# x1 and x2 turned by block loads and VectorE transposes instead of TensorE transposes, with two buffers of turned probability blocks and rounds that begin with the output projection

## The chip, the core and the metric

The kernel runs on one core of one Trainium2 chip, written in Bass with Tile. The core has five engines with an instruction stream each: TensorE (PE in the profile; PEld is its loading of weights), VectorE (DVE), ScalarE (ACT), GpSimd (POOL) and SyncE (SP). DMAs are issued from the streams of SP and ACT. The metric is device microseconds of one execution, as the median of a few executions.

## The reference

One decoder layer in float32, for 8 x 512 positions of width 512. `x` is (8, 512, 512); below, index t = 0..7 of the first axis is called a tile. Three blocks follow each other, each with a residual and a layer norm behind it:

```python
x = layernorm(x + self_attention(x))      # relative positions, 16 heads of 32, over the axis of 8
x = layernorm(x + cross_attention(ctx, x, mask))
x = layernorm(x + ffn(x))

# cross_attention, for each t: 8 heads of 64
k, v   = split((ctx[t] @ W_src.T + b_src) * mask[t])      # ctx[t]: 512 x 1024
q      = (x1[t] @ W_tgt.T + b_tgt) * mask[t]
p      = softmax(q k.T / 8, masked keys at -inf)          # 8 x 512 x 512
update = p v
return concat([x1[t], update]) @ W_out.T + b_out

# ffn: 512 -> 2048 -> 512
h   = relu(x2 @ w1.T + b1)
out = fp16(fp8(h) @ fp8(w2).T + fp16(b2))
```

Here `x1` is the output of the first layer norm and `x2` that of the second.

## The kernel before

**First stage, 0 to 928 us of the span.** Self attention over the axis of 8 for all positions, and beside it the projections of the contexts. It leaves the rows of x1 in DRAM (`x1d`, one array per tile, position by feature) and the keys and values of the tiles in DRAM (`kd`, `vd`). The context of the last tile is projected later, in the pieces `psk`/`psv` of `project_context`. The diff does not touch this stage.

**Second stage, 928 us to the end: rounds 0 to 7.** Each round works on a tile t and on the tiles behind it. In round t TensorE's stream holds, in this order of meaning:

- cross attention of tile t, in eight units u = (t, c, jj): c is one of four pairs of heads, jj one of two pairs of 128-row groups;
- output projection `project_out(t-1, j)`, j = 0..3, into the bank `pox`: four products of the turned x1 (`x1Ts`, two halves used in turn) and four of the turned attention output (`uT`), lines 890 and 894, then on VectorE the addition of the residual (the natural rows `x1`) and the statistics of the layer norm;
- `finish(t-2, j)`: the second product of the feed forward net (line 1045, bank `o`), additions, statistics, and in the side work the last normalization and the store of the result;
- the queries of tile t+1: `turn` transposes x1 on TensorE through PSUM (`xtr`, line 741) and ScalarE copies it into `x1Ts` (line 742); `queries(t+1, o)` multiplies it with `w_tgt` (line 747, bank `psq`), and VectorE writes `qTx` (line 754);
- the hidden layer of tile t-1, `hidden_steps`: x2 is transposed in the same way into `x2T` (`x2tr`), `sums_of_b` adds and subtracts its quarters on VectorE into `tx` (four additions), and then for n = 0..7 seven half-size products replace eight (groups `hx`, `hy`, `hz`, line 967, each of two weights and one 256-wide operand a piece). Results are added on VectorE (line 1002 after step `p13`, line 1012 after `p6`, line 1021 after `p7`) and copied or put through relu on ScalarE (lines 982, 988, 1008, 1015). The weights of the step n, with their sums, come from DRAM (`w1d`) into a ring of three: `load_w1`, issued on ACT's queue. For the first tile they come from `w1T` in parts on SP's queue, are summed on GpSimd and stored.

**A unit of cross attention.** `scores` (line 767) multiplies queries and keys for two j and two heads. Four `exponentials` follow: VectorE adds the mask and takes the minimum (line 786), ScalarE exponentiates and sums (line 796). Two `divide` (lines 808 and 811) scale on VectorE. Two `turn_blocks` (line 823) transpose on VectorE: each 32 x 32 block of `pe` is turned and put in its place in `pb`, a buffer of 128 x 4096 floats that the two units of one c share. That turns blocks in themselves; the blocks must still change partition. `move_blocks` (line 836) does this with sixteen DMAs on SP's queue, 128 KB each, from `pb` to `pT`. Then `attend` multiplies `pT` with the values (line 870, bank `av`), and ScalarE copies to `uT`. pb_c, av_c and vx_c below are the buffer, the attention and the values of the pair c. Both pools have one buffer:

```python
        pbp = pool("pb", 1)
        ptp = pool("ptp", 1)
```

**What sets the order.** PE, VectorE, ScalarE and SP run in the order in which the Python code issues instructions (`manual_schedule`). `weave` mixes two lists: `dense` (projections, queries, hidden layer; each item with a cost in us) and the attention of the round (`attention_of`: each item with a weight and with the number of dense items that must have gone before, `begun`, `projected`, `queried`). Side work, which is nearly all of VectorE's and ScalarE's part of the attention, stands in two lists, `side` and `urgent`. `run(cost, step)` is called for every item: it first issues the moves that are due, then takes side work as far as a credit of 0.7 of the costs allows, then issues the step. `settle(tag)` issues side work up to a tag at once. `later` holds loads that wait for some more items (keys `load_k`, values `load_v`). `attend` may be issued when its blocks are turned. `run` holds back the `turn_blocks` of the next pb while a move is due or was issued less than 15 modelled us ago:

```python
                held = moves or clock < moved + MOVE
                if held and any(item[0][0] == "t" for item in free):
                    free = [item for item in free if item[0][0] not in "tT"]
```

In `attention_of` the attention of the pair c stands behind the scores of unit 2c+3 of the same tile; that of the last pair stands in the next round, behind three of the `finish` steps:

```python
                    dense += first
                    begun = len(dense)
                    dense += values_of(t - 1) + second + out4[0]
```

So a round t from 2 to 6 begins with o_0 to o_2 of tile t-2, then the last attention of tile t-1, o_3, the four pox, the first attention of tile t, psq_0 to psq_2, the transposes of x2, psq_3, and the hidden layer, with scores in between and the other two attentions in the hidden layer. Natural x1 rows (`load_x1`, four buffers) are loaded a round ahead, at the beginning of the round. Round 0 has the context pieces, the turn of tile 1 and the queries of tile 1; round 1 begins with the last two pieces, psv_2 and psv_3, and `take_ring`, which reuses the memory of `w_src` for the weights of the hidden layer.

## Time and profile before

| | us |
|---|---|
| median of 3 executions (2267.41 to 2281.33) | 2270.61 |
| the profiled execution | 2276.34 |
| its span, first to last instruction | 2274.5 |
| first stage, to 928.0 | 928.0, PE busy 878.8 |
| round 0, 928.0 to 1080.6 | 152.6, PE busy 132.5 |
| round 1, to 1258.5 | 177.9, PE busy 147.3 |
| rounds 2 to 6, to 1414.5, 1565.7, 1718.7, 1871.9 and 2016.3 | 156.0, 151.2, 153.0, 153.2 and 144.4 |
| round 7, to 2158.8 | 142.5, PE busy 123.6 |
| the end, to 2274.5 | 115.7, PE busy 104.7 |

Each border from 1080.6 on is the start of the first pox of a tile in TensorE's stream (round 0 is what lies before the first of them, the end what follows the last tile's first pox; what a round has ahead of its first pox counts to the window before); a window's row of the trace gives each engine's busy time in it. Of the span of 2274.5 us PE is busy 2099.1, VectorE 1515.0, ScalarE 583.6, GpSimd 166.5. The mean granted clock of TensorE is 0.965 of full speed. DMA moved 293.31 MB in 141,247 packets.

How to read the profile: a group of instructions is given by line, engine, operation and its tiles, output before input (`pb<-pe` writes a tile of the name pb from one named pe), with its partitions and elements, its count, busy us and mean ns of one. Behind the bar stands the idle time of the engine just before those instructions and what ended most of it. A timeline's row is start, length, engine, line and operation, with the wait ahead of it and its releaser in brackets; SPq is the issuing of DMAs on SP. In the chain of waits each row is start, length, and the engine or DMA that the end was waiting for at that time. A row of the DMA view gives packets, MB and the share of 16 engines' time in the window asked for.

### The profile page before, as it was taken

The numbers are of one execution on the slowest core, as the hardware profiler recorded it, in microseconds if no ns is written. First come the engines' busy times: TensorE is split into PE (matmuls) and PEld (weight loads), VectorE is DVE, ScalarE is ACT, GpSimd is POOL, SyncE is SP. The second block draws the span as 40 slices with busy tenths as digits, with TensorE's granted clock in tenths as the row PEclk, the third lists the DMA queues.
The fourth block names the chain that finished last, engine by engine and source line by source line (L and its number), as shares of the span: only waits on it lengthen the run. The fifth ranks groups of instructions, "written<-read, shape, count | busy, mean of one in ns | idle before, by whom it ended". The sixth has DMA issues, their size and how long they took to land.

```text
span 2274.5 us, 21753 instructions
## 1 busy us (share of the span) xinstructions
PE 2099.1 (92%) x7552; PEld 1224.5 (54%) x7552; DVE 1515.0 (67%) x2542; ACT 583.6 (26%) x1327; POOL 166.5 (7%) x156
## 2 busy tenths in 40 slices
PE   7999999999989999888986999999989999998798
PEld 5654674465457667433354455464554654645455
DVE  4799999989999993356453654656646557456324
ACT  2011102111111111222242343342433433424312
POOL 1000110110001010102111000000000000000000
PEclk9999999999999999998998999999999999999899
DMA  8130452163035237554555444464453544634512
GB/s 297 48 126 13 153 178 77 37 220 102 7 121 176 83 125 261 191 165 116 136 140 169 107 136 119 116 187 117 121 168 87 140 134 111 177 92 130 138 49 86
DMA packets 141247, 293.31 MB, mean 129 GB/s; under 512 B 18640, under 2 KB 47312, under 8 KB 141136
## 3 DMA queue, kind: packets, MB, share of 16 engines
q1 hardware_dynamic: 116848, 211.91, 32.3%
q10 hardware_dynamic: 24288, 80.00, 10.7%
q8 instruction: 60, 0.98, 0.2%
q14 instruction: 51, 0.42, 0.1%
HBM read 165.49 MB, written 59.24 MB: 99 GB/s over the span
## 4 chain that ended last, share of the span: by engine, by line
PE 63%; DVE 19%; DMA 12%; ACT 2%; SPq 2%; issue 1%; POOL 0%; DVEq 0%; ACTq 0%; POOLq 0%
PE px L539 7%; PE hx L967 7%; PE av L870 5%; PE pox L890 5%; PE pox L894 5%; PE o L1045 4%; PE s L767 4%; PE pz L539 4%; DVE pv L428 3%; DMA ffn<-w1d 3%; PE psq L747 3%; PE hz L967 3%; PE ps_q L338 3%; DMA pT<-pb 2%; PE po L454 2%; DVE pv L438 2%
## 5 line engine op out<-in xcount | busy, mean ns | idle before, releaser
L796 ACT ACTIVATE pe<-pe,nmax 128x512 f32<-128x512 f32 x256 | 182.7, 715 | 350.9 <-DVE nmax L786 349.6
L823 DVE STREAM_TRANSPOSE pb<-pe 128x512 f32<-128x512 f32 x256 | 162.3, 681 | 86.7 <-DMA pT<-pb 64.2
L786 DVE CUSTOM_DVE_ANT_0 pe<-s,mb 128x512 f32<-128x512 f32 x256 | 163.5, 681 | 42.7 <-PE s L767 41.0
L967 PE MATMUL hx<-ffn 128*128 128x256 f32 x512 | 144.1, 406 | 49.9 <-DVE tm L1021 49.7
L428 DVE TENSOR_TENSOR pv<-v,sc 128x2048 f32<-128x2048 f32 x64 | 148.5, 2321 | 2.0
L967 PE MATMUL hx<-x2T,ffn 128*128 128x256 f32 x512 | 140.4, 398 | 8.4 <-ACT ffn L1008 8.4
L379 DVE TENSOR_TENSOR pq<-qw,k 128x2048 f32<-128x2048 f32 x64 | 146.3, 2286 | 1.1
L388 DVE TENSOR_REDUCE sc<-pq 128x64 f32<-128x2048 f32 x64 | 146.0, 2282 | 1.4
L870 PE MATMUL av<-pT,vx 128*64 128x512 f32 x512 | 127.1, 642 | 20.8 <-DMA pT<-pb 18.4
L967 PEld LDWEIGHTS hx<-ffn 128*128 128x128 f32 x512 | 94.9, 199 | 88.9 <-DVE tm L1021 59.0
L767 PE MATMUL s<-kT,qTx 64*128 64x512 f32 x512 | 128.7, 621 | 0.0
L811 DVE TENSOR_SCALAR pe<-pe,rden 128x512 f32<-128x512 f32 x256 | 119.5, 509 | 4.5
L967 PEld LDWEIGHTS hx<-x2T,ffn 128*128 128x128 f32 x512 | 98.6, 198 | 40.9 <-ACT ffn L1008 16.3
L454 PE MATMUL po<-w_o,aoT 128*128 128x512 f32 x256 | 118.6, 606 | 0.7 <-ACT aoT L451 0.7
L338 PE MATMUL ps_q<-w_in,xt 128*128 128x512 f32 x256 | 116.7, 593 | 0.0
L890 PE MATMUL pox<-w_xo,x1Ts 128*128 128x512 f32 x256 | 116.0, 596 | 0.0
L747 PE MATMUL psq<-x1Ts,w_tgt 128*128 128x512 f32 x256 | 113.5, 596 | 2.0 <-ACT x1Ts L742 2.0
L894 PE MATMUL pox<-w_xo,uT 128*128 128x512 f32 x256 | 115.1, 592 | 0.0
L338 PE MATMUL ps_k<-w_in,xt 128*128 128x512 f32 x256 | 114.0, 593 | 0.0
L1045 PE MATMUL o<-w2q,hq 128*128 128x512 fp8e4 x480 | 113.6, 397 | 0.0
L338 PE MATMUL ps_v<-w_in,xt 128*128 128x512 f32 x256 | 111.6, 594 | 0.0
L1002 DVE TENSOR_TENSOR ffn<-hx,ffn 128x256 f32<-128x256 f32 x64 | 27.2, 424 | 95.5 <-ACT hq L1015 66.6
(180 smaller groups left out, 3160.9 us busy)
## 6 DMA issues: line engine op xcount, KB each, us to landing
pT<-pb SPq DMA_DIRECT2D x512, 128.0 KB, 2.5
ffn<-w1d ACTq DMA_DIRECT2D x56, 896.0 KB, 5.7
ch<-in_ctxT_dram SPq DMA_DIRECT2D x56, 256.0 KB, 3.3
td<-tx SPq DMA_DIRECT2D x28, 384.0 KB, 3.3
tx<-td SPq DMA_DIRECT2D x28, 384.0 KB, 5.6
r<-in_x_dram SPq DMA_DIRECT2D x32, 256.0 KB, 3.8
xt<-in_xT_dram SPq DMA_DIRECT2D x32, 256.0 KB, 2.7
x1d<-r ACTq DMA_DIRECT2D x32, 256.0 KB, 3.9
```

The costliest lines, as they stand in the source:

```text
L338: nc.tensor.matmul(ps, lhsT=xt[:, e, :], rhs=w_in[:, e, part * E : (part + 1) * E], start=(e == 0), stop=(e == EC - 1),)
L428: nc.vector.tensor_tensor(pr, v_all[:, :, fs].rearrange("p s (h d) -> p s h d", d=D1), sc[:, t, g * HH * T : (g + 1) * HH * T] .rearrange( ...
L454: nc.tensor.matmul(po, lhsT=aoT[:, c * P : (c + 1) * P], rhs=w_o[:, c, :], start=(c == 0), stop=(c == EC - 1),)
L539: nc.tensor.matmul(bank[:, first], lhsT=w7[:, a, f, ps] if part == 0 else b[f][:, ps], rhs=b[f] if part == 0 else w7[:, a, f, :], start=st ...
L747: nc.tensor.matmul(ps, lhsT=w_tgt[:, e, o * P : (o + 1) * P], rhs=x1T[t][:, e, :], start=(e == 0), stop=(e == EC - 1),)
L767: nc.tensor.matmul(ps[:, h, :], lhsT=qT[t][half[h], c, j * P : (j + 1) * P], rhs=kT[t, c][half[h], :], start=True, stop=True,)
L796: nc.scalar.activation(pe, pe, AF.Exp, bias=nmax[:, h : h + 1], scale=-1.0, accum_out=den[:, h : h + 1],)
L870: nc.tensor.matmul(av[half[h], :], lhsT=v[t, c][:, s, half[h]], rhs=pT[t, c][:, :, :, s, h].rearrange("p g i q -> p (g i) q"), start=(s == 0),
L890: nc.tensor.matmul(po, lhsT=x1T[t][:, e, js], rhs=w_xo[:, e, :], start=(e == 0), stop=False)
L894: nc.tensor.matmul(po, lhsT=uT[t][:, e, js], rhs=w_xo[:, EC + e, :], start=False, stop=(e == EC - 1),)
L967: nc.tensor.matmul(ps[:, 0:W], lhsT=ring[:, (t * HH2 + n) % RING, a, e, :], rhs=b[:, e, :], start=start and e == 0, stop=e == 1, skip_grou ...
L1045: nc.tensor.matmul(po, lhsT=hq[t][:, c, j * P : (j + 1) * P], rhs=w2q[:, c, :], start=(c == 0), stop=(c == HC - 1),)
```

## The change

x1 and x2 get from rows to columns in another way. They are read from DRAM by DMAs that place 32 x 32 blocks where they belong, in runs of 32 floats, and VectorE then transposes every 32 x 32 block in place. x2 is stored to a new DRAM array for this. Only the last tile's x2 still goes through TensorE. `pb` has two buffers, `x1` two instead of four. The hold of `turn_blocks` and the two settles of the previous unit's transposes are gone. A round begins with the four pox, then come o_0 to o_3, the queries and the hidden layer; every attention stands directly ahead of the scores of the second-next unit, within its own round, and the natural rows of x1 are loaded in the middle of the hidden layer. The diff below leaves out most unchanged lines.

```diff
@@ -86,6 +86,7 @@
+    x2d = [dram.tile([NJ, P, E], F32, name=f"x2d{t}") for t in range(T)]
@@ -639,7 +640,7 @@
-        pbp = pool("pb", 1)
+        pbp = pool("pb", 2)
@@ -680,21 +675,13 @@
         def run(cost, step):
-            nonlocal credit, clock
+            nonlocal credit
             move()
-            clock += cost
             credit += 0.7 * cost
-            while credit > 0:
-                free = urgent + side
-                held = moves or clock < moved + MOVE
-                if held and any(item[0][0] == "t" for item in free):
-                    free = [item for item in free if item[0][0] not in "tT"]
-                if not free:
-                    break
-                q = urgent if urgent else side
-                q.remove(free[0])
-                credit -= free[0][1]
-                free[0][2]()
+            while credit > 0 and (urgent or side):
+                _, work, f = (urgent or side).pop(0)
+                credit -= work
+                f()
             credit = min(credit, 0.0)
             step()
@@ -719,13 +706,51 @@
             nc.gpsimd.tensor_scalar(mq, mbc, -1.0 / math.sqrt(D2), None, ALU.mult)
             mb[t] = mp.tile([P, S], F32, tag="mb", bufs=2, name=f"mb{t}")
             nc.gpsimd.tensor_scalar(mb[t], mbc, 0.0, MASKED, ALU.is_equal, ALU.mult)
-            x1T[t] = x1Ts[:, t % 2]
             qT[t] = qx.tile([P, EC, S], F32, tag="qT", bufs=2, name=f"qTx{t}")
             return mq
         def load_x1(t):
-            x1[t] = qx.tile([P, NJ, E], F32, tag="x1", bufs=4, name=f"x1{t}")
+            x1[t] = qx.tile([P, NJ, E], F32, tag="x1", bufs=2, name=f"x1{t}")
             nc.sync.dma_start(x1[t], x1d[t].rearrange("j p e -> p j e"))
+        def load_blocks(dst, src):
+            for a in range(4):
+                nc.sync.dma_start(
+                    dst[32 * a : 32 * a + 32].rearrange("p c (m e) -> p c m e", e=32),
+                    src.rearrange("j (g r) (c a e) -> a r c (j g) e", r=32, a=4, e=32)[a],
+                )
+        def turn_in_place(dst, c):
+            nc.vector.transpose(dst[:, c], dst[:, c])
+        def load_x1T(t):
+            x1T[t] = x1Ts[:, t % 2]
+            load_blocks(x1T[t], x1d[t])
+        def turn_x1(t):
+            for c in range(EC):
+                turn_in_place(x1T[t], c)
+        def load_x2T(t):
+            settle(("x2", t))
+            x2T[t] = qx.tile([P, EC, S], F32, tag="x2T", name=f"x2T{t}")
+            load_blocks(x2T[t], x2d[t])
+        def sums_of_x2(t):
+            b = [
+                x2T[t][:, 2 * i : 2 * i + 2, k * W : (k + 1) * W]
+                for i in range(2)
+                for k in range(2)
+            ]
+            sums_of_b(nc.vector, *b, *(tx[:, i] for i in range(3)))
+        def turn_x2(t):
+            for c in range(EC):
+                turn_in_place(x2T[t], c)
+            sums_of_x2(t)
         def load_k(t, c):
             kT[t, c] = kvd.tile([P, S], F32, tag="kT", name=f"kT{t}_{c}")
@@ -777,10 +802,6 @@
-                if i + h == (2 if t else 0):
-                    settle(("t", u - 1))
-                    settle(("T", u - 1))
@@ -850,16 +871,16 @@
-                side.append((("d", u), 1.2, lambda i=i: divide(i)))
+                side.append((u, 1.2, lambda i=i: divide(i)))
-                side.append((("t" if jj == 0 else "T", u), 1.3, lambda i=i: turn_blocks(i)))
+                side.append((u, 1.3, lambda i=i: turn_blocks(i)))
-                side.append((("T", u), 0.0, lambda: moves.append((u // 2, move_blocks))))
+                side.append((u, 0.0, lambda: moves.append((u // 2, move_blocks))))
-            settle(("T", (t * EC + c) * 2 + 1))
+            settle((t * EC + c) * 2 + 1)
@@ -905,14 +926,18 @@
+            def one(i):
+                y = x1[t][:, i, :]
+                normalize(y, y, mvb[t], rs[0], i)
+                if t < T - 1:
+                    nc.sync.dma_start(x2d[t][i], y)
-                y = x1[t][:, i, :]
-                urgent.append(
-                    (("x2", t), 0.7, lambda i=i, y=y: normalize(y, y, mvb[t], rs[0], i))
-                )
+                urgent.append((("x2", t), 0.7, lambda i=i: one(i)))
@@ -928,16 +953,14 @@
-        def turn_x2(t, j):
+        def turn_last_x2(j):
+            t = T - 1
-                xT2 = x2T[t]
-                b11, b12 = xT2[:, 0:2, 0:W], xT2[:, 0:2, W:S]
-                b21, b22 = xT2[:, 2:4, 0:W], xT2[:, 2:4, W:S]
-                sums_of_b(nc.vector, b11, b12, b21, b22, *(tx[:, i] for i in range(3)))
+                sums_of_x2(t)
@@ -1172,29 +1195,29 @@
-            for u in range(1, 2 * EC + 1):
-                if u < 2 * EC or t + 1 < T:
+            last = t + 1 == T
+            for u in range(1, 2 * EC + (1 if last else 2)):
+                if u % 2 == 1 and u > 1:
+                    f = lambda c=u // 2 - 1: attend_next(t, c)
+                    steps += [(3.8, projected, f, 0.05)]
+                if u < 2 * EC or (u == 2 * EC and not last):
-                    need = queried if u == 2 * EC else begun + (u > 1 or t == 0)
-                    steps += [[2.0, need, lambda n=n: scores(*n), 1.0]]
-                if u % 2 == 1 and u > (1 if t == 0 else 3):
-                    steps[-1][3] -= 0.7
-                    f = lambda c=u // 2 - 1: attend_next(t, c)
-                    weight = 2.2 if u == 2 * EC - 1 and t + 1 == T else 0.7
-                    steps += [(3.8, projected, f, weight)]
+                    need = queried if u == 2 * EC else begun
+                    steps += [(2.0, need, lambda n=n: scores(*n), 0.9 + 0.15 * (u % 2 == 0))]
+            if last:
+                steps[-1] = steps[-1][:3] + (2.2,)
-            load_x1(0)
+            load_x1T(0)
-            for j in range(NJ):
-                turn(x1T[0], x1[0], j, "xtr0")
+            turn_x1(0)
@@ -1202,17 +1225,9 @@
-                if t + 1 < T:
-                    mq = load(t + 1)
-                    load_x1(t + 1)
-                    turns = [
-                        of(0.6, lambda j=j: turn(x1T[t + 1], x1[t + 1], j, f"xtr{t + 1}"))
-                        for j in range(NJ)
-                    ]
-                    asked = [of(3.5, queries, t + 1, o, mq) for o in range(EC)]
-                    asked[0] = [(3.5, True, asked[0][0][2])]
-                else:
-                    turns = asked = [[]] * EC
+                mq = load(t + 1) if t + 1 < T else None
+                asked = [of(3.5, queries, t + 1, o, mq) for o in range(EC) if t + 1 < T]
+                asked = sum(asked, [])
@@ -1249,38 +1266,30 @@
...
-                    dense += sum(turns, []) + sum(asked, [])
+                    dense += of(0.0, turn_x1, 1) + asked
                     queried = len(dense)
                 else:
-                    def values_of(t):
-                        return of(3.8, attend_next, t, EC - 1)
                     out4 = [of(6.9, project_out, t - 1, j) for j in range(NJ)]
-                    done = [of(3.5, finish, t - 2, j, NJ) for j in range(NJ)]
-                    early = NJ if t + 1 < T else NJ // 2
-                    first = sum(done[: early - 1], [])
-                    second = done[early - 1]
+                    done = [of(3.5, finish, t - 2, j, NJ) for j in range(NJ) if t > 1]
                     if t == 1:
-                        first = of(6.9, pieces[-2])
-                        second = of(6.9, pieces[-1]) + of(0.0, take_ring)
-                    dense += first
-                    begun = len(dense)
-                    dense += values_of(t - 1) + second + out4[0]
-                    dense += out4[1]
-                    dense += out4[2] + turns[0] + turns[1] + out4[3]
+                        rest = of(6.9, pieces[-1]) + of(0.0, take_ring)
+                        done = [of(6.9, pieces[-2]), rest, [], []]
+                    dense += sum(out4, [])
                     projected = len(dense)
-                    dense += turns[2] + turns[3] + of(3.8, attend_next, t, 0) + asked[0]
-                    rest = asked[1:-1] if t + 1 < T else done[early:]
-                    dense += of(0.0, normalize_x2, t - 1) + sum(rest, [])
-                    for j in range(NJ):
-                        dense += of(0.6, turn_x2, t - 1, j)
-                    dense += asked[-1]
+                    dense += done[0] + of(0.0, normalize_x2, t - 1)
+                    if t + 1 < T:
+                        dense += of(0.0, load_x1T, t + 1)
+                    dense += done[1] + of(0.0, load_x2T, t - 1)
+                    dense += done[2] + done[3]
+                    if t + 1 < T:
+                        dense += of(0.0, turn_x1, t + 1)
+                    dense += asked[:2] + of(0.0, turn_x2, t - 1) + asked[2:]
                     queried = len(dense)
-                    dense += hidden_steps(t - 1)
+                    hidden = hidden_steps(t - 1)
+                    hidden[HC:HC] = of(0.0, load_x1, t)
+                    dense += hidden
                 weave(dense, attention_of(t, begun, projected, queried))
             last = of(3.5, finish, T - 2, 0, NJ) + of(3.8, attend_next, T - 1, EC - 1)
@@ -1289,7 +1298,7 @@
-                last += of(0.6, turn_x2, T - 1, j)
+                last += of(0.6, turn_last_x2, j)
```

More of the change, by code (lines that the diff above doesn't have):

```diff
@@ L654, in decoder_layer @@
         urgent, side = [], []
-        credit = clock = 0.0
-        moved = -99.0
-        MOVE = 15.0
+        credit = 0.0
         def settle(tag):
@@ L671, in move @@
         def move():
-            nonlocal moved
             while moves and moves[0][0] <= attended:
                 moves.pop(0)[1]()
-                moved = clock
             for item in later:
@@ L1223, in decoder_layer @@
                         qx.tile([P, FC // 2, S], F32, tag="x2T", name="ct7a"),
-                        qx.tile([P, FC // 2, S], F32, tag="x1", bufs=4, name="ct7b"),
+                        qx.tile([P, FC // 2, S], F32, tag="x1", bufs=2, name="ct7b"),
                     ]
@@ L1230, in decoder_layer @@
                         )
+                    load_x1T(1)
+                    load_x1(0)
                     pieces = project_context(
```

## The prediction

> **What bounds the kernel now.** First the page: its engine table, then the costliest groups with the idle time ahead of them.
>
> ```profile
> PE 2099.1 (92%) x7552; PEld 1224.5 (54%) x7552; DVE 1515.0 (67%) x2542; ACT 583.6 (26%) x1327; POOL 166.5 (7%) x156
> ...
> L823 DVE STREAM_TRANSPOSE pb<-pe 128x512 f32<-128x512 f32 x256 | 162.3, 681 | 86.7 <-DMA pT<-pb 64.2
> ...
> L967 PE MATMUL hx<-ffn 128*128 128x256 f32 x512 | 144.1, 406 | 49.9 <-DVE tm L1021 49.7
> ...
> L870 PE MATMUL av<-pT,vx 128*64 128x512 f32 x512 | 127.1, 642 | 20.8 <-DMA pT<-pb 18.4
> ```
>
> TensorE is the bound. Its largest single wait, 49.7 us, is for VectorE's L1021; VectorE in turn lost 64.2 us at L823, waiting until the one buffer pb was free. The chain of waits shows one such place (round t=4):
>
> ```profile
> 1531.88 6.66 DMA ffn<-w1d
> ...
> 1538.56 3.13 DMA pT<-pb
> ...
> 1541.95 1.30 DVE pb L823 x2
> 1543.26 0.32 DVE tm L1021
> ...
> 1543.62 2.07 PE hx L967 x4
> ```
>
> A weight load holds up the move of the blocks, the move holds pb, the transpose into pb holds VectorE, and the addition behind it in VectorE's order holds TensorE. Next the timelines, of TensorE, VectorE and SP:
>
> ```profile
> 1543.62 2.07 PE L967 MATMUL hx<-ffn 128*128 128x256 f32 x4 [3.44 <-DVE tm L1021]
> ...
> 1590.42 1.09 PE L741 MATMUL xtr<-ident,x 128*128 128x128 f32 x8
> ...
> 1602.88 10.10 SPq L836 DMA_DIRECT2D pT<-pb  x16
> ...
> 1615.09 1.91 PE L741 MATMUL x2tr<-ident,x 128*128 128x128 f32 x16
> ...
> 1635.33 17.14 SPq L836 DMA_DIRECT2D pT<-pb  x16
> ...
> 2096.66 1.29 DVE L823 STREAM_TRANSPOSE pb<-pe 128x512 f32<-128x512 f32 x2
> ...
> 2119.16 5.99 PE L870 MATMUL av<-pT,vx 128*64 128x512 f32 x16 [7.54 <-DMA pT<-pb]
> ...
> 2132.84 1.28 DVE L823 STREAM_TRANSPOSE pb<-pe 128x512 f32<-128x512 f32 x2
> ...
> 2153.56 5.35 PE L870 MATMUL av<-pT,vx 128*64 128x512 f32 x16 [4.13 <-DMA pT<-pb]
> ```
>
> Three readings. The transposes of x1 and x2 cost TensorE only some 3.8 us a round (8+8 at about 1.0 us each, 16 at 1.9). The sixteen DMAs of a move take 10.1 us to issue, but 17.1 while weights are loaded. From the end of the last transpose to the attention that waits for the blocks, round 7 has 2097.95 to 2119.16 = 21.2 us and 2134.12 to 2153.56 = 19.4, each with two weight loads on the way; round 0, without them, 1053.0 to 1067.5 = 14.5. I take 19.4 in the hidden layer. After a wait of over 2 us the next matmuls are slow (2.07 us for four instead of 1.03; an av 5.4 to 6.0 instead of 3.65): 1.7 us on top of each such wait.
>
> **Removed.** Rounds 3 to 5 last 152.5 us each (1414.5 to 1871.9). Leaving: 3.8 us of PE transposes; the waits for L1021, 25.5 us in rounds 3 to 6, so 6.4 a round, since with two pb a transpose waits only for the move before the last; and the slow matmuls behind its two waits, 3.4. Together 13.6 us. ScalarE loses 60 copies of 0.59 us, which is nothing on the path at 26% busy.
>
> **Added, the block loads.** Four DMAs a tile bring 8192 runs of 128 bytes. No row has this size; the nearest are in the DMA view: the last row loads of the setup on ACT's queue (60 bytes and less, window 6 to 7 us), and w1T's 512-byte rows (1081.5 to 1082.5).
>
> ```profile
> q10 hardware_dynamic: 218, 0.01, 16.5%
> ...
> q1 hardware_dynamic: 270, 0.13, 45.8%
> ```
>
> A share is of 16 engines over 1 us, so 16 x 0.165 / 218 = 12 ns a packet, and 16 x 0.458 / 270 = 27 ns. By size 128 bytes come to 14 ns: 8192 x 14 / 16 = 7.2 us a tile, between 6.1 and 13.8. The Trainium skill speaks against the change (DMA: Bandwidth & Descriptors, Specifications): below 512 bytes a DMA reads, modifies and writes. Priced as twice the 512-byte packet that is 54 ns, 27.6 us a tile. The 60-byte row shows no such penalty; I go by the row.
>
> Is 7.2 us hidden? Clock from the start of pox_0 in the changed order: pox (4 x 6.87) and one unit of scores (1.92) end at 29.4; av_0 33.0; o_0 36.5; scores 38.4; o_1 to o_3 48.8; psq_0 is next. The load of x1T waits at SP behind vx_2, which waits for av_0: issued at 33.7, landed by 33.7 + 7.2 + 2.5 = 43.4, in time. But its transposes stand in VectorE's order behind the addition and the statistics of o_3. VectorE has work ahead of that until 50.7, then 2.4 us (0.69 + 0.69 + 0.69 + 0.18 and gaps), then the first transpose: psq_0 starts at 53.8. **TensorE waits 5.0 us.** Behind the transposes on VectorE stand the division and transposes of pb_1, done at 59.7.
>
> x2 now goes out by four stores and comes back. The last normalization stands behind o_1's statistics and ends at 44.9; the store lands at about 48.6 (3.3 to 3.9 us for 256 KB), and only then does SP issue the blocks, which land near 58. VectorE reaches the turn after qTx of psq_1, at 63.5; TensorE needs it turned, with the first sum (3.2 us), at 69.6. Slack until the load takes 15.7 us, so the whole bracket is hidden. What queues behind it at SP is an output store (60.6), then the move of pb_1: 60.9 + 10.1 + 2.5 = 73.5 against av_1 at 73.1. I count 0.7.
>
> VectorE's 8 transposes (0.62 apart) come to 5 us a round, all in this stretch; beyond the 5.0 they stand under psq and hx.
>
> **Moved, the attentions.** This decides. Each attention now stands directly ahead of the second-next unit's scores, and the fourth ahead of the round's last scores; before, the fourth was held past three o. In the hidden layer the last transpose of pb_2 stands in VectorE's order behind the L1002 addition of n=2. From that product to av_2 the PE order has 15 groups of 0.865 and one scores, 14.9 us, with its small waits 15.4. Needed: 0.4 + 1.3 + 0.1 for addition and transposes, then 19.4 = 21.2. **av_2 waits 5.8.** For pb_3 the addition is that of n=6; 10 groups and one scores are 10.6, with small waits 11.1: **av_3 waits 10.1.** Nothing runs past them, as TensorE is in order. pb's second buffer doesn't help: pT has one, and the distance from scores to attention is short.
>
> Sum of a full round: -13.6 + 5.0 + 0.7 + 5.8 + 10.1 + 3 x 1.7 = +13.1. Rounds 2 to 6: +65.5.
>
> **The other rounds.** Round 0: VectorE turns tile 0 while TensorE ends the stage before, -3.3. But all four attentions now stand ahead of the first pox, each 14.5 us behind its transposes, and 14.1 us of psv work that covered them moves behind it. By the same stepping pox_0 starts at 1078, against 1080.6 with that work done: +11.6, say 12. Round 1: x2T's load stands at SP behind two load_w1, which last 8.0 and 8.9 us (1080.75 to 1097.95) and can't start before psv_3 frees the buffer; hz_0 waits about 16 us, and av_2 for loads of w1 on SP. Against it goes one 15 us wait on L1021. +8. Round 7 has no queries over the x2T load: a wait of about 11 instead of 5.5, and the two av waits stay: +7. The end keeps its PE transposes: 0.
>
> 12 + 8 + 65.5 + 7 = +92.5. The profiled execution took 2276.3 (span 2274.5 and 1.8 around it): 2368.8. It lies 5.7 above the median shown, 2270.6: **2363**.
>
> **Rivals.**
> *Moves at the pace of round 0* (14.5 us), since a waiting TensorE asks for no weights. av_2 waits 0.9, av_3 5.2, two slow starts: +1.6 a round; with round 7 at +3 the sum is +31, 2302. For it: 10.1 us moves in the trace. Against: both waits of round 7 had TensorE standing and still took 19 to 21. 12%.
> *Faster.* The freed 64.2 us of VectorE count and nothing follows. That needs blocks in place within 9.3 us of their last transpose (11.1 - 1.8). Then a round is -13.6 + 5.0 + 1.7 = -6.9, five are -34.5; rounds 0, 1 and 7 give about -21: 2215. Against: sixteen issues alone took 10.0 us at best. 10%.
> *Small packets are slow*, 54 ns: x1T lands at 63.3, 10 us late; x2T's load then starts behind it and ends 15 us later than needed: 25 a round more, with rounds 1 and 7 about +165: 2528. 8%.
> My own case: 70%.
>
> **Numbers.** The runs before span 2267 to 2281, so about 1% is what can be told from no change. My case's own range is 2310 to 2420 (14.5 to 21.2 us a move, 6.1 to 13.8 a tile). The range, 2275 to 2425, takes in the slow-pace rival, and leaves out the faster one and the slow packets. Slower by over 1%: 80% (mine, the packets, a little of the first rival); within 1%: 10% (the rest of it); faster: 10%.
>
> **What would show it.** L823 waiting for DMA pT<-pb near zero; the av group's idle time grown from 20.8 to well over 80 us, put down to DMA pT<-pb, about 6 and 10 a round; psq waiting some 5 us a round on VectorE's turn; x1Ts<-x1d landing within 8 to 12 us; full rounds of about 165 us. It is wrong if av doesn't wait or the block loads take over 16 us.

## The result and the profile after

| | before | changed |
|---|---|---|
| median of 4 executions, us | 2271.93 | 2414.72 |
| the profiled execution and its span | 2276.34, 2274.5 | 2413.56, 2411.8 |
| PE busy, us | 2099.1 | 2098.5 |
| mean granted clock | 0.965 | 0.938 |

The changed kernel takes 1.0625 times as long (1.0589 to 1.066): 142.8 us more, where the forecast had 92.4 (2363 less the 2270.6 shown then). The time lies in the forecast's range, 10 us under its upper end. The spans differ by 137.3 us. TensorE's busy time is the same in sum, so the net loss is waiting; within the sum slow matmuls (av 163.2 us instead of 127.1) took the place of the transposes that left. First the page of the changed kernel, its engine table and the groups that answer to those of before:

```profile
PE 2098.5 (87%) x7312; PEld 1200.7 (50%) x7312; DVE 1547.3 (64%) x2602; ACT 554.3 (23%) x1267; POOL 166.2 (7%) x156
...
L891 PE MATMUL av<-pT,vx 128*64 128x512 f32 x512 | 163.2, 795 | 156.8 <-DMA pT<-pb 122.2
...
L844 DVE STREAM_TRANSPOSE pb<-pe 128x512 f32<-128x512 f32 x256 | 161.5, 683 | 0.0
...
L772 PE MATMUL psq<-x1Ts,w_tgt 128*128 128x512 f32 x256 | 124.7, 644 | 24.7 <-DVE x1Ts L727 24.7
...
L990 PE MATMUL hx<-ffn 128*128 128x256 f32 x512 | 136.4, 389 | 0.8 <-DVE tm L1044 0.5
```

VectorE no longer waits for pb (86.7 us of idle ahead of the transposes became 0.0), and TensorE no longer for the third addition (49.9 became 0.8). In their place the attention waits 156.8 us for its blocks, where it waited 20.8, and one av matmul takes 795 ns instead of 642: slow starts.

Now the same round t=4 as in the prediction. Timelines of TensorE, VectorE and SP (start, length, engine, line, and the wait ahead):

```profile
1682.46 6.58 PE L772 MATMUL psq<-x1Ts,w_tgt 128*128 128x512 f32 x8 [4.64 <-DVE x1Ts L727]
...
1706.87 1.13 PE L990 MATMUL hz<-x2T,ffn 128*128 128x256 f32 x4 [2.77 <-ACT tm L1011]
...
1744.77 6.09 PE L891 MATMUL av<-pT,vx 128*64 128x512 f32 x16 [4.59 <-DMA pT<-pb]
...
1784.99 6.46 PE L891 MATMUL av<-pT,vx 128*64 128x512 f32 x16 [9.11 <-DMA pT<-pb]
```

```profile
1681.69 2.49 DVE L727 STREAM_TRANSPOSE x1Ts<-x1Ts 128x512 f32<-128x512 f32 x4
...
1725.57 1.29 DVE L844 STREAM_TRANSPOSE pb<-pe 128x512 f32<-128x512 f32 x2
```

```profile
1662.55 6.59 SPq L721 DMA_DIRECT2D x1Ts<-x1d  x4
...
1726.89 15.18 SPq L857 DMA_DIRECT2D pT<-pb  x16
...
1766.17 16.97 SPq L857 DMA_DIRECT2D pT<-pb  x16
```

Four places make the round. The queries wait 4.64 us for VectorE's turn of x1, the first hz 2.77 us, av_2 4.59 and av_3 9.11. A move issues its sixteen DMAs in 15 to 17 us, and from the last transpose into pb (ends 1726.86) to av_2 (1744.77) are 17.9 us. Behind each wait but the short one at hz, the next group is slow (6.58 us for eight matmuls instead of 3.7, an av 6.09 and 6.46 instead of 3.65).

By rounds, from one first pox to the next, with the products that the new order carries over a border put back (psv_2 and psv_3, 14.1 us, and o's of 3.46 us each), the change of the profiled execution is:

| | forecast | changed kernel |
|---|---|---|
| round 0 | +12 | +27.7 |
| round 1 | +8 | +24.4 |
| rounds 2 to 6, sum | +65.5 | +67.7 |
| round 7 | +7 | +17.8 |
| the end | 0 | -0.4 |

The full rounds came as forecast, 13.5 us each against 13.1. The three odd rounds were underrated by 43 us together.

### The profile page after: what moved, and what is told of

It is laid out like the page before. It is cut to its first block, busy times and chain, and to the rows that moved or that the text cites. A ratio compares the mean times of both kernels' runs of the same rounds, so it can differ in the third digit from the quotient of the medians.

```text
span 2411.8 us, 21441 instructions
## 1 busy us (share of the span) xinstructions
PE 2098.5 (87%) x7312; PEld 1200.7 (50%) x7312; DVE 1547.3 (64%) x2602; ACT 554.3 (23%) x1267; POOL 166.2 (7%) x156
## 4 chain that ended last, share of the span: by engine, by line
PE 59%; DVE 20%; DMA 12%; SPq 4%; ACT 3%; issue 2%; POOL 1%; ACTq 0%; DVEq 0%; POOLq 0%
PE av L891 7%; PE px L540 7%; PE hx L990 6%; DMA ffn<-w1d 5%; PE s L792 4%; PE pox L911 4%; PE pox L915 4%; DVE pv L429 3%; PE pz L540 3%; PE hz L990 3%; PE psq L772 3%; SPq L857 3%; PE ps_q L339 3%; PE po L455 2%; DVE pv L439 2%
## 5 line engine op out<-in xcount | busy, mean ns | idle before, releaser
L891 PE MATMUL av<-pT,vx 128*64 128x512 f32 x512 | 163.2, 795 | 156.8 <-DMA pT<-pb 122.2
L891 PEld LDWEIGHTS av<-pT,vx 128*64 128x64 f32 x512 | 48.2, 183 | 261.4 <-issue 244.9
L772 PE MATMUL psq<-x1Ts,w_tgt 128*128 128x512 f32 x256 | 124.7, 644 | 24.7 <-DVE x1Ts L727 24.7
L990 PE MATMUL hx<-ffn 128*128 128x256 f32 x512 | 136.4, 389 | 0.8 <-DVE tm L1044 0.5
L1035 DVE TENSOR_TENSOR ffn<-hz,ffn 128x256 f32<-128x256 f32 x64 | 27.2, 425 | 139.0 <-ACT ffn L1031 138.9
```

Source lines behind the costliest of these rows:

```text
L772: nc.tensor.matmul(ps, lhsT=w_tgt[:, e, o * P : (o + 1) * P], rhs=x1T[t][:, e, :], start=(e == 0), stop=(e == EC - 1),)
L891: nc.tensor.matmul(av[half[h], :], lhsT=v[t, c][:, s, half[h]], rhs=pT[t, c][:, :, :, s, h].rearrange("p g i q -> p (g i) q"), start=(s == 0),
L990: nc.tensor.matmul(ps[:, 0:W], lhsT=ring[:, (t * HH2 + n) % RING, a, e, :], rhs=b[:, e, :], start=start and e == 0, stop=e == 1, skip_grou ...
```

## Experiments

**The theories.** Theory 1 is the prediction's: attentions too close behind their scores, so that TensorE waits for the move of the blocks. Theory 2: the second pb is worth what its waits cost before, and more was lost elsewhere. Theory 3: the block loads slow the moves. The expectations number their rivals each for itself. All ratios are against the kernel before on the same chip.

**1. One pb again in the changed kernel.**

```diff
-        pbp = pool("pb", 2)
+        pbp = pool("pb", 1)
```

> The changed kernel with one pb again. Theory 1 (the attentions stand too close behind their scores, so TensorE waits for the move of the blocks): the second buffer buys next to nothing in this order, since the attention waits for the move anyway; full rounds 165 to 169 us as against 166, total 2405 to 2440 us; VectorE waits 60 to 100 us at the transposes, mostly while TensorE stands at an attention. Theory 2 (the second buffer is worth what its waits cost before, some 10 us a round, and the change lost more elsewhere): 2480 us or more, with the waits for the third addition of the hidden layer back.

Measured 2413.27 us against 2414.72, as theory 1 said. The page of this kernel:

```profile
L891 PE MATMUL av<-pT,vx 128*64 128x512 f32 x512 | 168.0, 816 | 156.3 <-DMA pT<-pb 111.5
L844 DVE STREAM_TRANSPOSE pb<-pe 128x512 f32<-128x512 f32 x256 | 161.5, 682 | 133.2 <-DMA pT<-pb 108.4
...
L990 PE MATMUL hx<-ffn 128*128 128x256 f32 x512 | 137.1, 390 | 11.7 <-DVE ffn L1025 10.8
```

VectorE waits 133.2 us for pb again and TensorE hardly notices (11.7 us ahead of hx, 10.6 of it once, in round 1), because it is standing at the attention for the same move. In this order the second buffer is worth nothing.

**2. x2 through TensorE, the rest of the change kept.**

```diff
-                    dense += done[1] + of(0.0, load_x2T, t - 1)
...
-                    dense += asked[:2] + of(0.0, turn_x2, t - 1) + asked[2:]
+                    dense += done[1]
...
+                    for j in range(NJ):
+                        dense += of(0.6, turn_last_x2, j, t - 1)   # between asked[:2] and asked[2:]
```

The store of x2 to `x2d` goes too.

> The changed kernel with x2 transposed on TensorE in every round (no x2d, no block loads of x2). Theory 1: the waits of av_2 and av_3 in a full round stay at 4.6 and 9.1 us; what goes is the wait at the first hz (18.6 us in round 1, some 5 of the 10 in round 7) and 1 to 2 us a full round after 1.9 us of added transposes: 2375 to 2400 us. Theory 3 (the block loads, through SP's queue and the DMA engines, are what slows the moves): the waits of av shrink by half or more, 2330 to 2350 us.

Measured 2360.94 us (1.0392), 54 less than the changed kernel and lower than I had expected. In rounds 2 to 6 av_2 still waits 5.2 us on average and av_3 8.9 (5.1 and 9.4 in the changed kernel), so the loads of x2 do not stretch the moves. What goes is the 18.6 us at the first hz of round 1 (the round is 21.0 us shorter) and 5.1 us in a full round: the 2.77 at hz, 1.0 of the wait at psq, and the rest fits fewer slow matmuls (PE busy in round 4 is 142.37 us instead of 144.44, although it now holds the transposes of x2). The edit does two things: the transposes of x2 also stand in the plan again with 2.4 us, where the turn stood with 0 (experiment 4). What of the 5.1 us is the work and what the plan, no run here separates.

**3. The order alone.** x1 and x2 through TensorE, one pb, four buffers of x1, rows loaded a round ahead; attention placement, the round's order and `run` without the hold as in the changed kernel.

```diff
-                    if t + 1 < T:
-                        dense += of(0.0, load_x1T, t + 1)
...
-                        dense += of(0.0, turn_x1, t + 1)
+                    dense += turns          # of(0.6, turn(...)) for j in 0..3
...
```

> The order of the changed kernel alone: x1 and x2 through TensorE, one pb, four buffers of x1, attention directly ahead of the second-next unit's scores, rounds that begin with the output projection. Theory 1: nearly all of the loss is here: av_2 and av_3 wait some 5 and 9 us, full rounds 158 to 162 us as against 152.5 before and 161 with x1 alone by blocks; 2345 to 2365 us. Theory 3 (block loads): full rounds back to 153 to 155 us, 2290 us or less.

Measured 2326.05 us (1.0233): the order with the hold gone costs 54 us, less than theory 1 had (some 73 to 93) and more than theory 3 (18 at most). In its spans (50.0 us more than before) 25.9 us are in round 0, 14.6 in round 7 and only 6.9 in the five full rounds. Its round t=4, TensorE's timeline:

```profile
1692.34 5.35 PE L891 MATMUL av<-pT,vx 128*64 128x512 f32 x16 [4.09 <-DMA pT<-pb]
...
1731.78 6.14 PE L891 MATMUL av<-pT,vx 128*64 128x512 f32 x16 [5.22 <-DMA pT<-pb]
```

The waits are there, but the second is 5.2 and not 9.1 us. With experiment 2 between them, the 143 us of the change split into 54 for the order, 35 for x1 by blocks (with the second pb, which is worth nothing here) and 54 for x2 by blocks, when the parts are taken away in this sequence and each turn is counted with its price in the plan. Theory 3 is right that the block loads matter, though not by its mechanism, as experiments 2 and 4 show.

**4. The plan's price of the turns.** Why does av_3 wait longer when x1 comes by blocks? In the order-alone kernel 26 groups of the hidden layer lie between the scores of pair 3 and its attention in round 4, in the changed kernel 21. The weave counts costs: four transposes of x1 and four of x2 stood in it at 0.6 us each, the new turns at 0.0.

```diff
-                        dense += of(0.0, turn_x1, t + 1)
-                    dense += asked[:2] + of(0.0, turn_x2, t - 1) + asked[2:]
+                        dense += of(2.4, turn_x1, t + 1)
+                    dense += asked[:2] + of(2.4, turn_x2, t - 1) + asked[2:]
...
```

> The changed kernel in which the plan charges 2.4 us each for the turn of x1 and the turn of x2, as it charged for the four TensorE transposes, instead of nothing; the work is the same. If the side work on VectorE falls behind because the plan's cost, which gives it out, shrank: the last transposes of a unit come two products sooner, the waits of av_2 and av_3 fall from 5 and 9 to 3 and 5 us as in the kernel with the order alone, full rounds 158 to 161 us, 2375 to 2390 us. If contention of the block loads is what stretches them: 2405 to 2420 us.

Measured 2378.03 us (1.0458), 37 less with the same work. Round t=4 of this kernel, TensorE's timeline:

```profile
1671.73 6.58 PE L772 MATMUL psq<-x1Ts,w_tgt 128*128 128x512 f32 x8 [5.66 <-issue]
...
1728.38 5.35 PE L891 MATMUL av<-pT,vx 128*64 128x512 f32 x16 [3.85 <-DMA pT<-pb]
...
1767.08 6.66 PE L891 MATMUL av<-pT,vx 128*64 128x512 f32 x16 [4.48 <-DMA pT<-pb]
```

Pair 3 has its 26 groups again. The two waits fell from 13.7 to 8.3 us (8.4 on the mean of rounds 2 to 6, 7.6 with the order alone, 14.5 in the changed kernel), while the block loads and their traffic stayed; the wait of 2.77 us at hz is gone as well. Full rounds are 159.0 us instead of 166.5. So 7.5 of the 13.5 us a full round come from two prices in the plan; round 0, on the other hand, is 10 us longer.

**5. Fewer bytes of weights.**

```diff
-                nc.scalar.dma_start(w, w1d[n])
+                nc.scalar.dma_start(w[:, A11], w1d[n][:, A11])
```

> The changed kernel in which tiles 1 to 7 load one of the seven parts of the hidden layer's weights and leave out the other six (that part of the result is not computed from the right weights). If the weight loads are what stretches a move from 14.5 to 19 us: from the last transpose to av 12.5 to 14.5 us instead of 18, the waits of av_2 and av_3 down by 4 to 5 us each, full rounds 155 to 158 us instead of 166, total 2340 to 2370 us. If the sixteen issues alone set the pace: no change, 2405 to 2415 us.

Measured 2331.23 us (1.0261). Pair 3 in its round 4, SP and TensorE:

```profile
1728.35 10.25 SPq L857 DMA_DIRECT2D pT<-pb  x16
```

```profile
1740.39 6.57 PE L891 MATMUL av<-pT,vx 128*64 128x512 f32 x16 [2.34 <-DMA pT<-pb]
```

The move issues in 10.25 us instead of 16.97, and av_3 starts 12.0 us after the issue begins instead of 18.8; av_2 does not wait at all. Full rounds are 152.9 us instead of 166.5, a larger gain than I had expected. The weight loads on ACT's queue are what stretches a move.

**6. More side work on VectorE per step.**

```diff
-            credit += 0.7 * cost
+            credit += 1.0 * cost
```

> The changed kernel with one number changed: VectorE's side work is given out against the whole of the cost of each step instead of 0.7 of it, so a unit's transposes come sooner after its scores. If the time from the scores to the attention is short because the transposes are held back: the waits of av_2 and av_3 fall by some 4 us each, full rounds 158 us instead of 166, 2350 to 2370 us. If the distance on TensorE is too short whatever VectorE does: 2405 to 2415 us.

Measured 2344.58 us (1.0314), 70 less than the changed kernel and a little below the range: full rounds 158.3 us, av_2 waits 2.2 us and av_3 6.1, while psq waits 6.4 instead of 4.6. The time from scores to attention was also VectorE's pace, not TensorE's distance alone.

**7. The turn of x1 earlier on VectorE.**

```diff
+                    if t + 1 < T:
+                        dense += of(0.0, turn_x1, t + 1)
                     dense += done[2] + done[3]
-                    if t + 1 < T:
-                        dense += of(0.0, turn_x1, t + 1)
```

> The changed kernel with VectorE's turn of x1 issued ahead of o_2 instead of behind o_3's statistics. If psq waits for VectorE's queue and not for the landing: its wait of 4.6 us falls under 1 and the slow start behind it (6.6 us for eight matmuls instead of 3.7) goes, 5 to 7 us in each of rounds 2 to 6, 2375 to 2390 us. If the blocks land too late: VectorE stands at the turn, the statistics behind it are late, 2410 us or more.

Measured 2396.53 us (1.054), 18 less, half of what I expected. psq waits for nothing, with no slow start:

```profile
1668.97 3.60 PE L772 MATMUL psq<-x1Ts,w_tgt 128*128 128x512 f32 x8
```

So it was VectorE's queue and not the landing. But the work that was passed is late now: in rounds 2 to 6 an hx waits 1.6 to 2.2 us for the qTx of the last queries, and a full round gains 3.4 us, not 5 to 7.

**8. The attentions late.** The changed kernel, all parts kept, with the attentions in another place and other weights in the weave.

```diff
-                if u % 2 == 1 and u > 1:
-                    f = lambda c=u // 2 - 1: attend_next(t, c)
-                    steps += [(3.8, projected, f, 0.05)]
...
-                    steps += [(2.0, need, lambda n=n: scores(*n), 0.9 + 0.15 * (u % 2 == 0))]
+                steps += [(2.0, need, lambda n=n: scores(*n), ws[u - 1])]
+                if u in wa:            # 3, 5, 7: behind the scores, not ahead of them
+                    f = lambda c=u // 2 - 1: attend_next(t, c)
+                    steps += [(3.8, projected, f, wa[u])]
+            if not last:
+                steps += [(3.8, projected, lambda: attend_next(t, EC - 1), 0.05)]
```

with `ws = (.8, .8, .3, .7, .3, .6, .2, 1.4)` and `wa = {3: .7, 5: .4, 7: .7}` (2.2 for 7 in the last round).

> The changed kernel (block loads, two pb, output projection first) with the attentions moved away from their scores: each of the first three stands behind the scores of the second-next unit and some products more, the fourth at the end of the round with its scores brought forward by some 10 products. Theory 1: the waits of av_2 and av_3 fall from 5 and 9 to 0 to 3 us and their slow starts with them, full rounds 150 to 154 us instead of 166; rounds 0 and 1 keep most of their waits; 2315 to 2345 us. Rival (VectorE or SP is the limit in this order, the wait moves elsewhere): above 2385 us.

Measured 2263.36 us (three runs, 2253.24 to 2271.34; 0.9956, 0.9923 to 0.9989): level with the kernel before and 151 us less than the changed kernel, by the place of the attentions and of the scores that the weights move with them. That is more than I had expected, since round 0 gained too. Its round t=4:

```profile
1659.71 3.65 PE L891 MATMUL av<-pT,vx 128*64 128x512 f32 x16
...
1693.33 3.65 PE L891 MATMUL av<-pT,vx 128*64 128x512 f32 x16
```

No wait and no slow start at av_2 and av_3, though their moves take as long as ever: 17.8 and 18.3 us from the first issue to the last landing, as against 17.8 and 18.8 in the changed kernel. Full rounds are 149.7 us. psq still waits 4.3.

**9. The same with x2 through TensorE and the turn of x1 ahead of o_2** (the edits of 2, 7 and 8 together).

> The kernel with late attentions (block loads of x1, two pb, output projection first), with x2 through TensorE and the turn of x1 issued ahead of o_2. The waits of psq (4.3 us) and hz (2.2) and the slow starts behind them go, 2 us of transposes come: full rounds 144 to 146 us instead of 150, round 1 some 20 us shorter: 2200 to 2220 us, level with the earlier order with two pb (2213). If the late attentions were bought with VectorE's slack only: 2230 us or more.

Measured 2219.62 us (0.9765, 0.9741 to 0.9789). A full round waits 3.7 to 5.6 us in all and lasts 143.7 us.

**10. One pb in that kernel** (the edit of 1 on top of 9).

> The last kernel (late attentions, x2 through TensorE) with one pb instead of two. With the attentions directly ahead of the scores the second buffer was worth nothing (2413 against 2415 us). If it pays where the attentions stand late, since the next unit's transposes then come before the move is done: VectorE waits at the transposes and with it the additions of the hidden layer, 4 to 9 us a full round, 2245 to 2280 us. If one buffer is enough in any order that has no hold: 2215 to 2225 us.

Measured 2300.33 us (1.0127): 81 us more, and 20 above the range that I gave. First two groups of the page of experiment 9, then the same of this kernel:

```profile
L844 DVE STREAM_TRANSPOSE pb<-pe 128x512 f32<-128x512 f32 x256 | 161.3, 680 | 0.2 <-DMA pT<-pb 0.2
...
L987 PE MATMUL hx<-ffn 128*128 128x256 f32 x512 | 136.9, 390 | 5.0 <-DVE ffn L1022 4.5
```

```profile
L844 DVE STREAM_TRANSPOSE pb<-pe 128x512 f32<-128x512 f32 x256 | 161.3, 680 | 128.9 <-DMA pT<-pb 85.5
...
L987 PE MATMUL hx<-ffn 128*128 128x256 f32 x512 | 143.6, 405 | 53.4 <-DVE tm L1041 32.8
```

VectorE waits for pb as long as in experiment 1 (128.9 and 133.2 us), but now TensorE has work in hand that depends on VectorE: 53.4 us ahead of hx, where experiment 1 had 11.7 and experiment 9 has 5.0. The same buffer that was worth nothing with close attentions is worth 81 us with late ones. Neither order has the hold of `turn_blocks` that the kernel before had; what one buffer with the hold would do here was not run.

**11. The earlier order with two pb.** Order, attention placement and TensorE's transposes of the kernel before, `run` without the hold; two x1 buffers, the rows read into the free one for the transposes and once more for the residual; tiles 0 and 1 take the block loads.

```diff
+                    if t + 1 < T:
+                        dense += of(0.0, load_rows, t + 1)   # ahead of out4[1]
```

> The order of the kernel before (attention behind the second-next unit's scores, the last attention behind three o of the next round, pox after them), x1 and x2 through TensorE, but two pb and no hold of the transposes; to make room x1 has two buffers, with the rows read once for the transposes and once more for the residual, and tiles 0 and 1 take the block loads. Theory 1: the second buffer is worth the waits for the third addition and their slow starts, 10 us a full round, 15 in round 1: 2195 to 2230 us. Theory 2 (one pT is the limit, the second pb moves the wait to the attention): 2255 to 2280 us.

Measured 2238.0 us (0.9849, 0.9824 to 0.9875), less gain than I had expected. The waits for the third addition are gone, so the second buffer (with the hold gone, which was not run by itself) removes here what one buffer cost before, but each round has a new one for the rows that I load late. In round 4:

```profile
1568.57 1.97 PE L773 MATMUL xtr<-ident,x1r 128*128 128x128 f32 x8 [3.03 <-DMA x1r<-x1d]
```

**12. The same with the rows one projection sooner** (`load_rows` ahead of out4[0]).

> The earlier order with two pb again, but the rows for the transposes of x1 loaded one output projection sooner. The waits of the first transpose for its rows (2.7 to 4.2 us a round) and the slow starts behind them go: 4 to 5 us a round in six rounds, 2238 becomes 2205 to 2220 us. If the earlier stores on VectorE delay the additions of the output projection: 2235 us or more.

Measured 2212.7 us (0.9734, 0.9718 to 0.975), the fastest of all kernels here. Its page:

```profile
PE 2068.5 (94%) x7520; PEld 1201.7 (54%) x7520; DVE 1529.8 (69%) x2550; ACT 580.0 (26%) x1319; POOL 167.0 (8%) x156
```

Full rounds are 143.8 us (with the two o's put back that this order, like the earlier one, does later in round 6) and wait 3 to 4; the granted clock of round 4 is 1.00 where the changed kernel had 0.93.

## Why the prediction was right, and where it was not

The forecast of 2363 us is 52 us low. Of these, 43 are the three odd rounds, 2 the full rounds, and 7 the step from span to median: the profiled execution before lay 5.7 us above the median, the changed one 1.2 below. The range held, but not for the reason it was drawn: it was spread for the length of a move and the price of a packet, which both came out near their forecasts, while the odd rounds had no spread. That their error stayed inside it is luck.

**Right: what would bound.** The place of the attentions and the moves decide: 151 us go when attentions and scores are placed anew (experiment 8). pb's second buffer does not help in this order (1), and the moves are long because of the weight loads (5). The three rivals did not come: the moves did not fall to round 0's pace though TensorE stood (17.9 and 18.8 us in round 4), VectorE's freed time bought nothing by itself, and small packets were not slow (below).

**Right: the terms of a full round.** Means of rounds 2 to 6 against the forecast: psq 4.64 us (5.0), av_2 5.1 (5.8), av_3 9.4 (10.1), av_1 0 (0.7), from the last transpose to av_2 and av_3 17.9 and 18.8 in round 4 (19.4). The block load of x1 was forecast at 9.7 us with its landing. It was issued at 1662.55 and the last of its four DMAs landed at 1674.1, after 11.5 us and still 7.6 us before VectorE's turn. The DMA view of the changed kernel, windows 1666 to 1668 and 1672 to 1674, shows what a packet costs and when the packets end:

```profile
q1 hardware_dynamic: 2098, 0.27, 97.9%
...
q1 hardware_dynamic: 361, 0.55, 102.6%
```

The first window is nothing but runs of 128 bytes: 16 x 2 x 0.979 us / 2098 = 14.9 ns each, forecast 14. In the second they run out, some 10 us after the issue (98 of its 361 packets are under 512 bytes). The estimate of 54 ns, which I had made from the rule of the Trainium skill (DMA: Bandwidth & Descriptors, Specifications) by doubling the 512-byte packet, is not what a packet took.

**Mis-sized: the slow starts.** 1.7 us each were taken. In round 4 they are 2.9 at psq (6.58 - 3.7), 2.4 and 2.8 at the two av, but that round is a bad one: on the mean of rounds 2 to 6 they are 2.2, 2.3 and 2.3, so the term of 5.1 us is 6.8. With it the added time is 4.6 + 1.8 (hz) + 14.5 + 6.8 = 27.7 us where 26.7 were forecast; the net of 13.5 means that 14.2 left where 13.6 were forecast. Among what left, two slow hx were priced at 1.7 us each too, though the row shown with the forecast has 1.0 (2.07 instead of 1.03). Nor is the limit of 2 us sharp: in the kernel before, hx ran at full speed behind a wait of 2.21 us and slowly behind one of 2.43.

**Wrong: x2 "hidden".** The landing was hidden as worked out, but the forecast took that for the whole cost. x2 by blocks, with its price of 0 in the plan, costs 5.1 us a full round (2). VectorE and ScalarE in round 4:

```profile
1695.29 2.48 DVE L727 STREAM_TRANSPOSE x2T<-x2T 128x512 f32<-128x512 f32 x4
```

```profile
1702.33 1.28 ACT L817 ACT_TABLE_LOAD   x1 [20.30 <-DVE nmax L807]
...
1706.46 0.35 ACT L1011 COPY tm<-hz 128x256 f32<-128x256 f32 x1
```

VectorE's turn waits for nothing, but with the sums it stands ahead of its own part of a unit's exponentials; ScalarE waits for that part, loads a table (1.28 us), exponentiates four times and only then copies hz, and hz waits 2.77 us (0.99 before). I had stepped TensorE and the loads and not ScalarE behind VectorE. The turn does this only in the plan's order of the changed kernel: with the prices back (4) x2 still comes by blocks, and in the full rounds hz does not wait.

**Half right: "This decides".** The place of the attentions decides, but the new order is only part of what put them there. With the transposes on TensorE the same order loses 1.4 us a full round (3). 7.5 us of the loss come from the prices of the turns in the plan (4), which moved the scores and the side work. The forecast took the positions from the changed order as it stands, so its number held, but it did not see which part of the diff made them.

**Wrong: round 0, +27.7 for +12.** Four attentions wait there, av_1 5.3 us and the others as in TensorE's timeline:

```profile
978.49 5.24 PE L891 MATMUL av<-pT,vx 128*64 128x512 f32 x16 [12.53 <-DMA pT<-pb]
...
1052.71 5.67 PE L891 MATMUL av<-pT,vx 128*64 128x512 f32 x16 [11.79 <-DMA pT<-pb]
...
1068.44 3.78 PE L792 MATMUL s<-kT,qTx 64*128 64x512 f32 x8 [4.51 <-DVE nmax L807]
1086.47 5.86 PE L891 MATMUL av<-pT,vx 128*64 128x512 f32 x16 [14.24 <-DMA pT<-pb]
```

and VectorE's, between the last two attentions:

```profile
1062.05 0.75 DVE L779 SCALAR_TENSOR_TENSOR qTx<-psq,colv,mq 128x512 f32<-128x512 f32 x1 [17.57 <-PE psq L772]
```

The forecast gave each pair 14.5 us from its transposes. The last three took 15.0, 12.0 and 12.2, so that was not short. What it lacked is VectorE's order: the qTx of psq_3 stands ahead of the next unit's division and transposes, psq_3 stands behind av_2 on TensorE, and av_2 waits 11.8 us. VectorE stood 17.6 us, so the transposes of the last pair ended at 1074.3, and av_3 waited its 14.2 with nothing to hide it. The first move also took 16.9 us to issue beside the loads of the context and of x1 (20.7 us to the attention).

**Wrong: round 1, +24.4 for +8.** The wait at hz was 18.6 us (16 forecast). VectorE at its end, and SP's queue:

```profile
1176.58 2.49 DVE L727 STREAM_TRANSPOSE x2T<-x2T 128x512 f32<-128x512 f32 x4 [22.36 <-DMA x2T<-x2d]
```

```profile
1145.38 0.38 SPq L974 DMA_DIRECT2D ffn<-in_w1T_dram  x1
...
1164.46 7.21 SPq L721 DMA_DIRECT2D x2T<-x2d  x4
```

The step that failed is the one after it: "and av_2 for loads of w1 on SP" was named without a number. Measured on TensorE:

```profile
1235.98 2.08 PE L990 MATMUL hy<-x2T,ffn 128*128 128x256 f32 x4 [8.52 <-DMA ffn<-in_w1T_dram]
...
1267.20 2.08 PE L990 MATMUL hy<-x2T,ffn 128*128 128x256 f32 x4 [6.37 <-DMA ffn<-in_w1T_dram]
...
1288.18 5.70 PE L891 MATMUL av<-pT,vx 128*64 128x512 f32 x16 [10.44 <-DMA pT<-pb]
```

Two hy wait for w1T (in the kernel before five such waits came to 8.1 us in all). The first load stands on SP behind a move of 11.1 us. The second stands behind a store of summed weights, which SP can issue at 1256.7 only, since GpSimd first adds a bias to the rows of x1 (5.0 us) that the changed kernel loads in the middle of the hidden layer. And av_3 waits 10.4, which the forecast priced in full rounds and left out here.

**Wrong: round 7, +17.8 for +7.** hz waited 10.0 (11 forecast), and av_2 and av_3 11.2 and 5.6 as against 7.5 and 4.1. Left out was av_1. TensorE in the changed kernel, then in experiment 2:

```profile
2212.76 5.91 PE L891 MATMUL av<-pT,vx 128*64 128x512 f32 x16 [9.28 <-DMA out_dram<-x]
```

```profile
2155.21 5.06 PE L891 MATMUL av<-pT,vx 128*64 128x512 f32 x16 [7.85 <-DMA out_dram<-x]
```

(The store named as releaser was issued right behind the move, whose last block landed at 2212.5 in the changed kernel.) The transposes of av_1 stand on VectorE behind the turn of x2, which waits 4.0 us for its landing. That is the smaller part: with x2 through TensorE av_1 still waits 7.9 us. This round has no queries between the scores and av_1, only 13 groups of the hidden layer (some 11 us), so the distance is short here too; the forecast reckoned with the missing queries at hz alone.

The failures have much in common: I stepped TensorE, and VectorE only at the instruction in question. In rounds 0 and 1 most of the missing part stood behind an instruction on VectorE, SP or GpSimd that waits or is long; in rounds 1 and 7 an attention was left out whose distance is short as well.

## What to carry to other kernels

A second buffer pays only where the engine that matters has something else to do while the first is in use: here it was worth 0 us with consumers close behind their producers, and 81 us with consumers late (both without a hold of the producer), so move the consumer first and then add the buffer. When work leaves a scheduler's list or its price is set to nothing, the plan around it moves; here two prices of 2.4 us made 37 us. And when an instruction waits, write down what stands behind it on its own engine in each round, the odd rounds above all: in a strict order that is where the next wait is.

## What the runs showed of the hardware

A 32 x 32 block gather in runs of 128 bytes took 14.9 ns a packet in a window that held nothing else, 133 GB/s. A packet of 512 bytes took 27 ns, so a small run costs less by the packet and about twice as much by the byte. Its four DMAs hold the issuing queue for 5.1 to 7.6 us from round 1 on, and the four of round 0, issued right behind the loads of `w_src` and the context, for 16.5. The sixteen DMAs of a move hold it for 10 us, and for 15 to 18 with weight loads on the other queue. The cost of a wait on TensorE is not its length alone: in rounds 2 to 6 of the changed kernel, behind waits of 4.6 to 10.6 us, the next eight to sixteen matmuls took 1.5 to 3.0 us more, and the granted clock of a round is 0.93 (22 us of waits) where experiment 12 has 1.00 (3 us).
